# Three ScalarE instructions and eight matmuls at other steps of a hand-written step table (layer 2 of a four-layer image kernel)

## Chip, cores, metric

The kernel runs on one core of one Trainium2 chip. The metric is the device time of one execution in microseconds (us). The kernel before takes 7983.3 us (median of three runs, 7979.73 to 7997.88).

## What is computed

An image of 2 x 64 x 96 x 96 numbers (fp32) goes through four layers. Layer 0 is a non-local attention block over the 9216 positions, layer 3 a filter whose taps depend on the image's mean. Between them stand five selective state-space scans ("Mamba" blocks): one in layer 1, over each image as one sequence, and four in layer 2. Layer 2 has two halves; each runs a forward and a backward block over the image's rows or columns as short sequences of 96:

```python
def _block(u, p):
    return _mamba(_rmsnorm(u, p['norm_w']), p) + u
def _bimamba(u, pf, pb):
    yf = _block(u, pf)
    yb = jnp.flip(_block(jnp.flip(u, 1), pb), 1)
    return jnp.concatenate([yf, yb], axis=-1)
...
# in _mamba: x = silu(conv(in_proj(u))); dt, B, C from x; then over time, per channel d and state s:
h = dA * h + dt_t[:, :, None] * B_t[:, None, :] * x_t[:, :, None]   # dA = exp(dt * A)
y = einsum('nds,ns->nd', h, C_t)
```

The norm of layer 2 is x times the inverse root of the mean of its squares over 64 channels. The forward and the backward block of a pair read the same normalized image.

## The kernel before

**Units and steps.** Layers 1 and 2 are cut into 120 units of 768 positions: 24 units of layer 1, then 96 of layer 2, which come in 48 pairs, a forward and a backward unit of the same eight sequences. The first 24 pairs are layer 2's first half, the others its second. A unit's states, 128 channels by 16 states, take 16 steps; a step handles 128 rows in two turns of 384 positions. The first eight steps are the unit's first 384 positions, the other eight its second, so a unit has two "halves" of B.

**One step** (`run`, from L955). SyncE issues two transfers of 384 KB that spread rows of dt and of dt times x over the partitions (`read`, L846), five steps ahead. ScalarE makes the decay, two exponentials of 128x384 (`decay`, L853), three steps ahead. VectorE multiplies the spread rows by B into PSUM (`inputs`, L863; two steps' worth at every even step) and runs the scan (`scan`, L878). GpSimd multiplies the states by C (L879). TensorE sums the states into y (`gather`, L888), two steps behind or more. Below, "placement s" is L863 of step s, "product s" is L879 of step s.

**B.** One PSUM bank holds B for one half (`shared`, L857). The matmul of the second half is recorded in step 6, behind placements 6 and 7, which are the last to read the first half's B; that of the next unit's first half in step 14, behind placements 14 and 15.

**The step table.** Everything else of a unit is a list of pieces, `PIECES` (L930): (offset in steps from the unit's start, method). The pieces of later units run between the steps of the one being scanned. In every step, `run` records first the reads, the decay, the placement and scan, `shared` and the gathers, then the pieces that are in `reads` (L961), then the others, each group in the table's order. What is recorded is the order of each engine's queue: the whole runs under a manual schedule. Buffers come from pools; a piece that needs a new buffer waits until the old one's last reader is done. One two-bank PSUM buffer (`m`) serves all pieces of TensorE in turn.

**The pieces around the change**, with the step at which each falls and the unit that is then being scanned:

| piece | line | engine, work | step |
|---|---|---|---|
| `norm_square`, layer 2 | L714, L715 | ScalarE: two copies of the image (64x768 each, to both halves of the partitions), one square of 128x768 | 15 of a forward unit, for the pair after next; in `reads` |
| `norm_mean`, `norm_root` | L693, L723 | TensorE mean, ScalarE log and exp | 1 and 3 of a backward unit |
| `norm_scale` | L737 | GpSimd | 10 of a backward unit |
| `conv` | L755, L761 | TensorE: four taps by two halves, 16 records | 5, every unit, for the unit after next |
| `conv_read` | L766 | ScalarE | 7 |
| `gate_mm`, `gate_read` | L693, L772 | TensorE, ScalarE | 7, 9 |
| `y_half` | L892 | ScalarE: copy of the first half of y | 10 |
| `silu` | L775, L776 | ScalarE: table load, silu, table load | 10 |
| `tail_0`, `tail_1`, `tail_read` | L671, L924 | TensorE: the previous pair's output, ScalarE copies it to the image | 9, 10, 11 of a forward unit |
| `step_mm`, `step_read`, `step_exp` | L671, L792 to L799 | TensorE, ScalarE: towards dt of the next unit | 11, 13, 14 |
| `step_kept`, `step_sum`, `step_dt`, `step_u` | L806 to L816 | GpSimd: dt and dt times x | 15, 1, 5, 7 |
| `step_write` | L825 | SyncE: two transfers of 768 KB, the rows of the next unit | 8 |

SyncE's queue holds `step_write` between the reads of step 13 and those of step 14: `read` runs five steps ahead, and `step_write` is recorded in step 8 after that step's reads. Layer 1 has its own form of the norm (`u.carry`), one per unit.

Of the kernel before, what the change touches and what calls it, by code (L numbers as in the profile page):

```python
# [20 lines left out]
AF = mybir.ActivationFunctionType  # L21
# [10 lines left out]
D_STATE, DT_RANK, D_CONV = 16, 4, 4  # L32
HALF = 4 * W
CH = 2 * HALF
# [33 lines left out]
def rows_of(b):  # L68
    return slice(b * C, (b + 1) * C)
# [551 lines left out]
class Mamba:  # L621
# [79 lines left out]
            u.p = self.mm([(self.t.centre[rows_of(u.b)], self.halves(u.image))])  # L701

    def norm_square(self, u):
        if u.norm.unit is not u:
            return
        u.norm.x = self.work("xn", D_CONV - 1 + CH)
        u.sq = self.work("sq", bufs=1)
        x = u.norm.x[:, D_CONV - 1 :]
        if u.carry:
            self.nc.scalar.activation(u.sq, u.p, AF.Square)  # L710
            self.nc.scalar.copy(x, u.p)
        else:
            for j in range(2):
                self.nc.scalar.copy(x[rows_of(j)].rearrange("p (n t) -> p n t", n=u.image.shape[1]), u.image)  # L714
            self.nc.scalar.activation(u.sq, x, AF.Square)  # L715

    def norm_mean(self, u):
        if u.norm.unit is u:
# [197 lines left out]
    def tail_read(self, u):  # L916
# [10 lines left out]


    PIECES = (
        (-51, "norm_centre"),  # L930
        (-49, "norm_square"),
        (-47, "norm_mean"),
        (-45, "norm_root"),
        (-38, "norm_scale"),
        (-36, "norm_affine"),
        (-27, "conv"),
        (-25, "conv_read"),
        (-25, "gate_mm"),
        (-23, "gate_read"),
        (-22, "silu"),  # L940
        (-21, "step_mm"),
# [25 lines left out]
    def run(self, units, first, n_first, other):  # L967
# [8 lines left out]
        table = [[] for _ in range(self.STEPS)]  # L976
        for offset, name in self.PIECES:
            table[offset % self.STEPS].append((name not in reads, offset, name))
        begin, end = self.PIECES[0][0], self.PIECES[-1][0]


        self.nc.scalar.preload_act_table_set("natural_log_exp_and_others")
        first(0)
        for offset, name in self.PIECES:
            if offset < 0:
# [326 lines left out]
```

## Time and profile before

| | busy us | share of 7974.9 us |
|---|---|---|
| TensorE | 7063.0 | 89% |
| VectorE | 6749.1 | 85% |
| ScalarE | 5214.3 | 65% |
| GpSimd | 4724.4 | 59% |

These shares mix stages. Layer 0 takes about the first 2700 us; layer 1's units are scanned from 2732 to 3821 us, layer 2's from 3821 to 7890 us, layer 3 is the rest. From 5882 to 7890 us VectorE is busy 1934.15 of 2008 us, GpSimd 1825.96, TensorE 1697.87, ScalarE 1511.72, and the 16 DMA engines have a mean share of 0.90. So in layer 2 VectorE sets the pace, and what it waits for is what can be gained. The unit of account in the text below is the pair: two units, some 84 us, 48 times.

A row of the timeline is: start, duration, engine, line, operation, tiles written and read, form, count; then the engine's idle time before it, and who ended it.

### The profile page before, as it was taken

The page shows a single profiled execution, that of the slowest core. Times are in us where ns is not written, and L with a number is a line of the kernel's source. Part 1 is how long each engine was busy: PE and PEld are TensorE (multiplying, and loading weights), DVE is VectorE, ACT ScalarE, POOL GpSimd, SP SyncE. Part 2 cuts the span into 40 slices and gives each one's busy share as a digit, 9 for nine tenths or more (in the row PEclk, how much of TensorE's full clock was granted, in tenths as well). Part 3 has the DMA queues.
Part 4 walks back from the last instruction along what each step waited for, and adds up shares of the span by engine and source line. Part 5 has one row for each costly group of instructions (what it writes and reads, how often), then busy time and mean ns, then how long its engine had stood idle before and what let it go on. Part 6 is the DMA issues. An engine that isn't in the chain of part 4 may idle for free.

```text
span 7974.9 us, 82275 instructions
## 1 busy us (share of the span) xinstructions
PE 7063.0 (89%) x24578; PEld 3122.4 (39%) x24578; DVE 6749.1 (85%) x5524; ACT 5214.3 (65%) x6953; POOL 4724.4 (59%) x3146
## 2 busy tenths in 40 slices
PE   9999999999999788888888888888888888888887
PEld 3333333333333344444444444444444444444443
DVE  6666666666666599999999999999999999999999
ACT  4444444444444577777777777777777777777773
POOL 0000000000000399999888889989889999999985
PEclk9999999999999899999999999999999999999999
DMA  1000000000000388888888888988998899898985
GB/s 43 1 1 1 1 1 1 3 5 5 5 5 3 144 303 317 312 304 325 312 332 325 328 329 329 342 334 328 334 337 334 340 341 347 336 336 335 343 335 205
DMA packets 593806, 1726.06 MB, mean 216 GB/s; under 512 B 65988, under 2 KB 67140, under 8 KB 592840
## 3 DMA queue, kind: packets, MB, share of 16 engines
q1 hardware_dynamic: 591904, 1717.68, 57.9%
q8 instruction: 196, 3.21, 0.2%
q10 hardware_dynamic: 1448, 3.05, 0.1%
q14 instruction: 258, 2.11, 0.1%
HBM read 1522.68 MB, written 197.79 MB: 216 GB/s over the span
## 4 chain that ended last, share of the span: by engine, by line
PE 11%; DMA 10%; ACT 9%; issue 8%; POOL 8%; DVE 4%; SPq 1%; DVEq 0%; ACTq 0%; POOLq 0%
DMA spread<-rows 7%; PE y L888 6%; POOL h L879 6%; ACT h L853 3%; DMA rows<-dtu 3%; PE mm L671 2%; DVE place L863 2%; DVE h L878 1%; PE conv L761 1%; POOL dtu L812 1%; POOL dtu L816 1%; PE y L885 1%; DVE xa L1211 1%; ACT xn L714 1%; PE mm L693 1%
## 5 line engine op out<-in xcount | busy, mean ns | idle before, releaser
L879 POOL TENSOR_TENSOR h<-h,C 128x768 f32<-128x768 f32 x1920 | 3452.4, 1817 | 347.4 <-DVE h L878 310.3
L888 PE MATMUL y<-h,pair 128*128 128x384 f32 x7680 | 2809.6, 510 | 103.4 <-POOL h L879 102.7
L878 DVE TENSOR_TENSOR_SCAN h<-h,place 128x768 f32<-128x768 f32 x1536 | 2606.3, 1737 | 13.6 <-ACT h L853 13.0
L888 PEld LDWEIGHTS y<-h,pair 128*128 128x128 f32 x7680 | 1513.6, 200 | 1306.8 <-POOL h L879 239.6
L311 ACT ACTIVATE e<-f_exp 128x1536 f32<-128x1536 f32 x864 | 1206.4, 1448 | 1224.4 <-PE f_exp L301 1224.4
L853 ACT ACTIVATE h<-spread,xa 128x384 f32<-128x384 f32 x3072 | 1734.3, 608 | 367.0 <-DMA spread<-rows 343.6
L367 DVE TENSOR_TENSOR acc_e<-acc_e,e 128x1536 f32<-128x1536 f32 x792 | 1389.9, 1755 | 683.7 <-ACT e L311 644.8
L863 DVE TENSOR_TENSOR place<-spread,B 128x768 f32<-128x768 f32 x1920 | 1735.0, 948 | 261.9 <-PE B L857 250.8
L340 POOL TENSOR_TENSOR xa<-xa,t_att 64x512 f32<-64x512 f32 x36 | 45.3, 1259 | 2612.3 <-ACT t_att L338 2612.3
L318 PE MATMUL y_att<-e,xb 128*64 128x512 f32 x5184 | 1243.7, 601 | 0.0
L301 PE MATMUL f_exp<-theta,phi 64*128 64x512 f32 x5184 | 1234.6, 607 | 1.0 <-DVE xb L284 0.5
L301 PEld LDWEIGHTS f_exp<-theta,phi 64*128 64x128 f32 x5184 | 466.4, 186 | 754.5 <-issue 460.6
L874 DVE TENSOR_TENSOR_SCAN h<-h,state,place 128x384 f32<-128x384 f32 x768 | 714.0, 990 | 0.0
L318 PEld LDWEIGHTS y_att<-e,xb 128*64 128x64 f32 x5184 | 341.6, 136 | 830.5 <-issue 829.2
L853 ACT ACTIVATE h<-spread,rates 128x384 f32<-128x384 f32 x768 | 433.0, 608 | 150.3 <-DMA spread<-rows 137.5
L885 PE MATMUL y<-raw,xa 128*128 128x384 f32 x384 | 220.4, 663 | 210.5 <-ACT yg L895 182.8
L671 PE MATMUL mm<-raw,xa 128*128 128x384 f32 x768 | 301.2, 517 | 99.2 <-ACT xb L924 91.5
L766 ACT ACTIVATE raw<-conv,cols 128x768 f32<-128x768 f32 x120 | 108.2, 902 | 305.2 <-PE conv L761 240.9
L806 POOL TENSOR_TENSOR kept<-dtu,kept 128x768 f32<-128x768 f32 x120 | 218.3, 1819 | 118.4 <-ACT kept L799 117.9
L761 PE MATMUL conv<-xn,xa 64*128 64x384 f32 (+3 forms) x1536 | 273.1, 494 | 11.7 <-DVE xa L1093 4.0
L892 ACT COPY yg<-y 128x384 f32<-128x384 f32 x120 | 57.4, 478 | 289.7 <-PE mm L671 205.1
L857 PE MATMUL B<-raw,xa 128*128 128x384 f32 x384 | 170.7, 526 | 83.8 <-DVE place L863 83.7
(206 smaller groups left out, 5434.3 us busy)
## 6 DMA issues: line engine op xcount, KB each, us to landing
spread<-rows SPq DMA_DIRECT2D x3840, 384.0 KB, 6.4
rows<-dtu SPq DMA_DIRECT2D x240, 768.0 KB, 5.9
image<-pre SPq DMA_DIRECT2D x11, 384.0 KB, 2.3
xb<-image SPq DMA_DIRECT2D x11, 384.0 KB, 5.8
xa<-in_x SPq DMA_DIRECT2D x1, 2304.0 KB, 23.1
out<-xa ACTq DMA_DIRECT2D x7, 240.0 KB, 2.0
out<-xa SPq DMA_DIRECT2D x1, 1200.0 KB
xa<-in_x SPq DMA_DIRECT2D x3, 384.0 KB, 11.6
```

The source lines that it names most:

```text
L301: nc.tensor.matmul(fs[j // 3][:, bass.ts(j % 3, NB)], lhsT=phi[at, bass.ts(m // 2, P)], rhs=theta[at, bass.ts(i, NB)], start=True, stop=True,)
L311: nc.scalar.activation(e, f, AF.Exp)
L318: nc.tensor.matmul(y[rows_of(m % 2)], lhsT=g[:, m, :], rhs=es[j // 3][:, bass.ts(j % 3, NB)], start=m < 2, stop=m >= KEYS - 2,)
L367: nc.vector.tensor_add(acc, acc, e)
L671: self.nc.tensor.matmul(o, lhsT=lhsT, rhs=x, start=n == 0, stop=n == len(terms) - 1)
L761: self.nc.tensor.matmul(p3[:, :, o], lhsT=lhsT, rhs=x3[:, :, i], **flags)
L853: self.nc.scalar.activation(h[:, bass.ts(q, HALF)], dt, AF.Exp, scale=u.w.rates[:, n : n + 1])
L863: self.nc.vector.tensor_mul(bx, x, self.B.unsqueeze(1).to_broadcast([P, 2, HALF]))
L874: nc.vector.tensor_tensor_scan(h[:, at], h[:, at], bx[:, at], state[:, q : q + 1], ALU.mult, ALU.add)
L878: nc.vector.tensor_tensor_scan(h[:, way], h[:, way], bx[:, way], 0.0, ALU.mult, ALU.add)
L879: nc.gpsimd.tensor_mul(h2, h2, u.C[:, bass.ts(half, HALF)].unsqueeze(1).to_broadcast([P, 2, HALF]))
L888: self.nc.tensor.matmul(self.y, lhsT=self.t.gather[n], rhs=rhs, start=False, stop=stop)
```

## The change

```diff
     def norm_square(self, u):
-        if u.norm.unit is not u:
-            return
-        u.norm.x = self.work("xn", D_CONV - 1 + CH)
-        u.sq = self.work("sq", bufs=1)
-        x = u.norm.x[:, D_CONV - 1 :]
         if u.carry:
+            u.norm.x = self.work("xn", D_CONV - 1 + CH)
+            u.sq = self.work("sq", bufs=1)
             self.nc.scalar.activation(u.sq, u.p, AF.Square)
-            self.nc.scalar.copy(x, u.p)
-        else:
-            for j in range(2):
-                self.nc.scalar.copy(x[rows_of(j)].rearrange("p (n t) -> p n t", n=u.image.shape[1]), u.image)
-            self.nc.scalar.activation(u.sq, x, AF.Square)
+            self.nc.scalar.copy(u.norm.x[:, D_CONV - 1 :], u.p)
+
+    def image_copy(self, u, j):
+        if u.norm.unit is u and not u.carry:
+            x = u.norm.x[rows_of(j), D_CONV - 1 :].rearrange("p (n t) -> p n t", n=u.image.shape[1])
+            self.nc.scalar.copy(x, u.image)
+    def image_0(self, u):
+        if u.norm.unit is u and not u.carry:
+            u.norm.x = self.work("xn", D_CONV - 1 + CH)
+        self.image_copy(u, 0)
+    def image_1(self, u):
+        self.image_copy(u, 1)
+    def image_square(self, u):
+        if u.norm.unit is u and not u.carry:
+            u.sq = self.work("sq", bufs=1)
+            self.nc.scalar.activation(u.sq, u.norm.x[:, D_CONV - 1 :], AF.Square)
...
     PIECES = (
+        (-56, "image_0"),
+        (-52, "image_1"),
+        (-52, "image_square"),
         (-51, "norm_centre"),
...
-        (-27, "conv"),
-        (-25, "conv_read"),
-        (-25, "gate_mm"),
+        (-26, "conv"),
+        (-24, "conv_read"),
+        (-24, "gate_mm"),
         (-23, "gate_read"),
```

For layer 2, the first image copy goes from step 15 of a forward unit to step 8 of the same unit, the second copy and the square to step 12; all three now stand behind that step's `reads` pieces. For every unit, the convolution goes from step 5 to step 6, where `shared` is recorded before it; its read and the gate's matmul go from step 7 to step 8. `gate_read` stays in step 9. No instruction is added or taken away. On TensorE's queue the order "gather 3, convolution, B, gather 4" becomes "gather 3, B, gather 4, convolution"; on ScalarE's the copy and the square of step 12 stand between the decay of step 12 and that of step 13, ahead of `step_read` and `step_exp`. The first copy of the first layer-2 pair takes a buffer whose last reader is `norm_scale` of the last layer-1 unit, which GpSimd does in step 10, two steps after the copy's own.

## The prediction

> **What bounds the kernel now.** I first looked at the busy time by stretch: in layer 2 VectorE is busy 96% of the time, so I read who ends its waits there (waits of VectorE, 3821 to 7890 us: who, for whom, total us, times, longest):
>
> ```profile
> DVE place L863 <- PE B L857: 137.1, 84, 3.2
> DVE h L878 <- ACT h L853: 13.0, 17, 1.7
> DVE place L863 <- DMA spread<-rows: 9.6, 16, 1.1
> ```
>
> Nearly all is placement waiting for B. Sorted by step over VectorE's timeline, 57.7 us stand before placement 0 of backward units, 73.4 us before placement 8 of backward units, 6.0 us before placement 8 of forward ones. Two waits per pair, then, with different causes. I follow the pair that starts at 5288.96; A is its forward unit, B its backward unit, scanned from 5331.50. VectorE:
>
> ```profile
> 5331.50 1.82 DVE L863 TENSOR_TENSOR place<-spread,B 128x768 f32<-128x768 f32 x2 [2.32 <-PE B L857]
> ...
> 5353.98 1.83 DVE L863 TENSOR_TENSOR place<-spread,B 128x768 f32<-128x768 f32 x2 [2.31 <-PE B L857]
> ```
>
> Without a wait two steps take 5.02 us (from one placement pair to the next), a unit 40.2. TensorE in the same pair:
>
> ```profile
> 5303.25 2.82 PE L761 MATMUL conv<-xn,xa 64*128 64x384 f32 x16
> 5305.99 0.91 PE L857 MATMUL B<-raw,xa 128*128 128x384 f32 x2
> ...
> 5324.98 2.35 PE L671 MATMUL mm<-raw,xa 128*128 128x384 f32 x4 [1.92 <-ACT xb L924]
> 5327.12 3.69 PE L888 MATMUL y<-h,pair 128*128 128x384 f32 x8
> 5330.65 0.81 PE L857 MATMUL B<-raw,xa 128*128 128x384 f32 x2
> ...
> 5350.29 2.81 PE L761 MATMUL conv<-xn,xa 64*128 64x384 f32 x16
> 5353.03 0.91 PE L857 MATMUL B<-raw,xa 128*128 128x384 f32 x2
> ```
>
> The wait at placement 8 (5353.98) is the convolution in front of B: it is worth 2.74 us (start of `conv` to start of `B`). The wait at placement 0 (5331.50) has another cause: `step_mm` waits for `tail_read`, and the gathers and B stand behind it. In A the convolution costs nothing: it fills the time until placement 7, which B must wait for, ends at 5305.81. ScalarE and GpSimd:
>
> ```profile
> 5317.63 0.48 ACT L892 COPY yg<-y 128x384 f32<-128x384 f32 x1 [5.04 <-PE mm L671]
> 5323.36 1.57 ACT L924 ACTIVATE xb<-mm,cols 64x768 f32<-64x768 f32 x1
> 5328.22 0.89 ACT L793 ACTIVATE dtu<-mm,cols 128x768 f32<-128x768 f32 x1
> 5331.75 0.94 ACT L799 ACTIVATE kept<-kept,minus 128x768 f32<-128x768 f32 x1
> 5333.73 3.11 ACT L714 COPY xn<-xb 64x768 f32<-64x768 f32 x2
> 5367.48 0.61 ACT L853 ACTIVATE h<-spread,xa 128x384 f32<-128x384 f32 x1 [0.78 <-DMA spread<-rows]
> ```
>
> ```profile
> 5332.77 1.82 POOL L806 TENSOR_TENSOR kept<-dtu,kept 128x768 f32<-128x768 f32 x1 [1.57 <-ACT kept L799]
> 5335.12 3.60 POOL L879 TENSOR_TENSOR h<-h,C 128x768 f32<-128x768 f32 x2 [0.54 <-DVE h L878]
> 5356.53 0.11 POOL L820 MEMSET dtu<- 128x8 f32 x1
> ```
>
> `y_half` stood idle 5.04 us for TensorE's tail, so everything of ScalarE behind it in A (silu, `tail_read`, `step_read`, `step_exp`) hangs on when TensorE reaches the tail. GpSimd's `kept` waits for the end of `step_exp`, and from its first product in B to the end of `step_u` it does not pause. Only then does SyncE issue the rows (5356.67), and behind them the reads of steps 14 and 15; the last of these lands 10.8 us later, when ScalarE's row of 5367.48 starts. Placement 15 needs that transfer; here it starts at 5369.92 and does not wait, because the wait at placement 8 has pushed it back by 2.31 us.
>
> [...] `kept` idles 1.57 us at the head of GpSimd's queue with products behind it. [...] behind 1.92 us of waiting, 12 matmuls from 5324.98 take 5.67 us (start to start of B), against 0.32 us each in steady gathers.
>
> **The change, part by part** (durations from the pair above; the sum is made against the profiled span of 7974.9 us, 8.4 below the median of the three runs).
>
> 1. *B ahead of the convolution, in B units.* B no longer waits for 2.74 us of convolution. The 73.4 us go, and the 6.0 us of forward units.
>
> 2. *The same in A units.* TensorE gets there at 5303.25, that is A+14.29, but B must wait for placement 7 until A+16.92. The convolution that filled this time now comes after it. From `conv` to `y_half` TensorE's packed work is 13.53 us in this half of layer 2 where no wait falls in it (14.38 in this pair, two waits for GpSimd within), 12.91 in the second half; its contents do not change. So `y_half` comes at A+16.92+13.53 = 30.45, against 28.67: 1.8 later. Over all pairs `y_half` is now at A+28.9 (first half) and A+29.2 (second, where the earliest possible becomes 29.8): on average 1.5 and 0.7 later, a little more where TensorE comes later than 16.92.
>
> 3. *First copy at step 8 of A.* 1.45 us in the first half, 0.83 in the second, on ScalarE between `conv_read` and the decay. It is hidden in the 5.04 us before `y_half`. `gate_read`, now one step behind its matmul, falls into the same idle time. In B units and in layer 1 `y_half` may come 0.5 to 1.5 us later; there ScalarE then waits for transfers (2 to 3 us before the decay of step 14 in layer 1), which hides it: nothing.
>
> 4. *Second copy and square at step 12 of A.* 1.56+0.84+0.03 = 2.43 us (first half), 1.74 (second), ahead of `step_read` and `step_exp`, less 0.3 to 0.7 of ScalarE's waits for transfers that they fill. Behind them on the queue: the decays of steps 0 and 1 (slack of some steps), `step_read`, `step_exp`; who waits for these: GpSimd's `kept`, and all its products behind it.
>
> 5. *What they leave at step 15:* ScalarE no longer has 3.95 us of copies between the decays of steps 2 and 3 of B. The 13.0 us of waits for the decay go. `y_read` and `norm_mean` stay about where they are, since the same work now stands earlier.
>
> **The sum.** End of `step_read` in A: 30.45 + 5.73 (to `tail_read`, as now) + 1.59 + 1.1 (decay) + 2.43 + 1.1 + 1.68 = 44.08, against 40.15. The end of `step_exp` follows 3.58 later as now: 47.66, against 43.73. GpSimd: 23.4 from there to the rows' issue (seen in every backward unit where `kept` is late): 71.1, against 67.7. Last transfer of step 15: 10.2 to 10.8 later, 81.3 to 81.9; then 0.12, and 4.18 from placement 15 to the next pair: 85.6 to 86.2. The pair takes 85.0 on average now (pairs 11 to 24, from the start of one to that of the next), so 0.6 to 1.2 more. The wait at placement 8 is thus replaced by two: a longer one at placement 0 of B, and a new one at placement 15 of B for the rows. Second half, with its terms: 29.83 + 5.77 + 0.97 + 1.1 + 1.74 + 1.1 + 1.68 + 3.58 + 23.4 + 10.2 to 10.8 + 4.3 = 83.7 to 84.3 where TensorE is in time at A+16.92, against 83.74 on average; as it often isn't (the convolution starts at A+16.07 on average, and up to 18.4), I add 0.3. I take 0.9 for 14 pairs, 0.7 for 24, and 0.5 for the first ten, where VectorE's own weight preparation (2.7 us a pair) hides some: 12.6 + 16.8 + 5 = 34 us.
>
> Once, at the border of the layers, the first copy waits for GpSimd's `norm_scale` two steps on: ScalarE stands still for up to 10 us in layer 1's chain. Bounds: 0, if its later waits for transfers (3 us a unit) and slack take it up, and 12; a gain is excluded, since nothing gets earlier. I take 8. Sum 42 us: 7983.3 + 42 = 8025.
>
> The unknown: whether the pause of TensorE before B in A (0 to 2.6 us, new) drops its clock. Between nothing[...] and 1.9 us (six matmuls at 0.64) in half the forward units, 48/2 x 1.9 = 46 us. I take nothing; the upper end goes into the range.
>
> **Rivals.** *The rows have slack* (ends faster): if `step_exp` ends by B+2.0, the rows land before placement 15 would come, and the 79.4 + 13.0 us of waits are simply gone, less what placement 0 gains: 7983 - 92 = 7891, or 7930 if the 1 us at placement 0 stays on (48 x 0.8). For it: in some pairs now (B units with no wait at 8) the rows are in time. Against: there `step_exp` ends at B+1.0, and the change puts it some 3.9 us later (43.73 to 47.66), of which a later start of B takes back about 1. The point from which it decides is B+2.0. Chance 0.15. *It cancels*: the pair stays at its length within 0.3 us, 7983 +- 16. For it: the least values of the sum above (85.5 and 83.5) give 14 x 0.5 - 24 x 0.2, nearly nothing. Chance 0.17. *Clock*: the pause drops TensorE's clock, 8025 + 46 = 8071. Chance 0.13. My forecast, the rows' chain: 0.55.
>
> **The numbers.** 8025 us is the likeliest case, alone 7999 to 8060. A measurement of this kernel can tell 0.2% (16 us) from no change. Faster 0.15, same 0.17, slower 0.55 + 0.13 = 0.68. The range leaves out most of the faster case and the far end of the clock's: 7955 to 8080.
>
> **What would show it.** Right: no wait for B at placement 8; waits for B at placement 0 of backward units of 2 to 3 us on average; a new wait of 1 to 2.5 us for `spread` at placement 15 of backward units; `kept` ending 1 to 2 us later in B; layer 1 as before. Wrong: the rows issued before B+25.7, no wait at placement 15, and `y_half` of A before 29.8.

## The result and the profile after

The changed kernel takes **8027.6 us** (median of four runs, 8027.27 to 8042.47), the kernel before 7981.5 on the same chip: a ratio of 1.0058, 95% interval 1.0040 to 1.0075. It is 46 us slower. The profiled executions have spans of 7974.9 and 8026.0 us, 51 us apart; the sums by stage and by step below are of these two. Below, A+18.2 is a time 18.2 us after the start of the forward unit A of a pair.

First the waits of all engines in layer 2 (engine, line, who ended the wait: us, times, longest), cut to the rows that answer to those of before. The lines of the changed kernel lie 14 further down: placement is L877, the decay L867, B L871.

```profile
ACT h L867 <- DMA spread<-rows: 415.3, 885, 3.6
...
DVE place L877 <- DMA spread<-rows: 133.2, 134, 3.6
...
DVE place L877 <- PE B L871: 70.8, 43, 3.4
...
DVE h L892 <- ACT h L867: 7.9, 9, 2.1
```

VectorE's waits for B fell from 137.1 to 70.8 us, and its waits for transfers rose from 9.6 to 133.2. ScalarE's decays waited 343.3 us for transfers before and 415.3 now. Sorted by step over VectorE's timeline: the 79.4 us at placement 8 are gone, as are the 13.0 us at scan 3; 69.6 us of waits for B stand before placement 0 of backward units (57.7 before); and of the waits for transfers 77.9 us fall in backward units (74.3 of them at placements 14 and 15) and 55.3 in forward ones, against 0.8 and 8.9. With the scan's waits for the decay, VectorE waits 212 us for these three, against 160: the 52 us more are about what layer 2 grew by (54 us to the start of its last unit).

VectorE in one pair (A starts at 5481.02, B at 5525.03; same columns as in the prediction):

```profile
5518.19 0.96 DVE L877 TENSOR_TENSOR place<-spread,B 128x768 f32<-128x768 f32 x1 [1.04 <-DMA spread<-rows]
5521.39 1.75 DVE L892 TENSOR_TENSOR_SCAN h<-h,place 128x768 f32<-128x768 f32 x1 [0.59 <-ACT h L867]
5525.03 1.83 DVE L877 TENSOR_TENSOR place<-spread,B 128x768 f32<-128x768 f32 x2 [1.89 <-PE B L871]
5561.81 0.96 DVE L877 TENSOR_TENSOR place<-spread,B 128x768 f32<-128x768 f32 x1 [1.50 <-DMA spread<-rows]
5564.12 0.96 DVE L877 TENSOR_TENSOR place<-spread,B 128x768 f32<-128x768 f32 x1 [1.35 <-DMA spread<-rows]
```

No wait is left at placement 8. The wait at placement 0 is there as before, and the transfers are late in both units, not in B alone. TensorE in the same pair:

```profile
5490.42 1.65 PE L899 MATMUL y<-raw,xa 128*128 128x384 f32 x2 [5.20 <-ACT yg L909]
...
5499.25 0.81 PE L871 MATMUL B<-raw,xa 128*128 128x384 f32 x2
5501.28 2.82 PE L775 MATMUL conv<-xn,xa 64*128 64x384 f32 x16
...
5520.21 1.56 PE L671 MATMUL mm<-raw,xa 128*128 128x384 f32 x4 [1.90 <-ACT xb L938]
5524.18 0.81 PE L871 MATMUL B<-raw,xa 128*128 128x384 f32 x2
```

B now precedes the convolution. It comes at A+18.2 and not at A+16.9: TensorE has waited 5.20 us for `y_read` (L909) before it (265.6 us of such waits in layer 2, 182.8 before). ScalarE and GpSimd, through the pair:

```profile
5512.87 0.48 ACT L906 COPY yg<-y 128x384 f32<-128x384 f32 x1 [3.29 <-PE mm L671]
...
5518.60 1.55 ACT L938 ACTIVATE xb<-mm,cols 64x768 f32<-64x768 f32 x1
5520.18 1.12 ACT L867 ACTIVATE h<-spread,xa 128x384 f32<-128x384 f32 x2
5521.32 1.56 ACT L716 COPY xn<-xb 64x768 f32<-64x768 f32 x1
5522.92 0.84 ACT L729 ACTIVATE sq<-xn 128x768 f32<-128x768 f32 x1
5523.67 1.10 ACT L867 ACTIVATE h<-spread,xa 128x384 f32<-128x384 f32 x2
5524.80 0.90 ACT L806 ACTIVATE dtu<-mm,cols 128x768 f32<-128x768 f32 x1
...
5529.13 0.94 ACT L813 ACTIVATE kept<-kept,minus 128x768 f32<-128x768 f32 x1
...
5560.81 0.61 ACT L867 ACTIVATE h<-spread,xa 128x384 f32<-128x384 f32 x1 [1.71 <-DMA spread<-rows]
5561.71 0.61 ACT L867 ACTIVATE h<-spread,xa 128x384 f32<-128x384 f32 x1 [0.29 <-DMA spread<-rows]
5563.02 0.61 ACT L867 ACTIVATE h<-spread,xa 128x384 f32<-128x384 f32 x1 [0.70 <-DMA spread<-rows]
...
5565.98 0.62 ACT L867 ACTIVATE h<-spread,xa 128x384 f32<-128x384 f32 x1 [0.30 <-DMA spread<-rows]
5566.50 0.88 ACT L806 ACTIVATE dtu<-mm,cols 128x768 f32<-128x768 f32 x1
...
5570.82 0.94 ACT L813 ACTIVATE kept<-kept,minus 128x768 f32<-128x768 f32 x1
```

```profile
5530.15 1.82 POOL L820 TENSOR_TENSOR kept<-dtu,kept 128x768 f32<-128x768 f32 x1 [5.11 <-DVE h L892]
5531.92 3.59 POOL L893 TENSOR_TENSOR h<-h,C 128x768 f32<-128x768 f32 x2
...
5551.41 1.83 POOL L830 TENSOR_TENSOR dtu<-dtu,raw 128x768 f32<-128x768 f32 x1
5553.31 0.11 POOL L834 MEMSET dtu<- 128x8 f32 x1
```

Read these two fences as one **closed loop**. In A, the tail's copy (5518.60), the second image copy and the square stand one behind the other ahead of `step_read` (5524.80). `step_exp` ends at 5530.07, B+5.04. GpSimd's `kept` follows at once (5530.15; its row names a scan, which ended at the same moment, but in all 47 pairs measured `kept` starts 0.08 us behind the end of `step_exp`), and GpSimd is done with the rows at 5553.42. SyncE issues them at 5553.44. The rows need two transfers of 3.03 us each (the median from the landing of one transfer to that of the next), and every read behind them 0.98 us. That is why ScalarE's six decays of 5560.81 to 5566.6 wait for one transfer after the other: steps 14 and 15 of B, and step 0 of the next unit. `step_read` of the next A stands behind them (5566.50). So `step_exp` ends at 5571.76, which is 3.46 us into the next A. It ended near A+0.9 in this half of layer 2 before. From there the late `step_exp` delays A's own rows, and also the copy of y (`y_read`, A+8.9 against A+6.4), and with that TensorE's next gathers (the 5.20 us above), its convolution and its tail. Then the turn begins again. From the end of `step_exp` that falls in A (5484.53) to the one that falls in B it takes 45.54 us, and from there to the one in the next A 41.69: together 87.2, about the length of this pair. The sum alone proves no loop, since whatever comes once a pair recurs after a pair's length. That the links have no slack, and so set this length, is for the experiments to show.

### The profile page after: what moved, and what is told of

Its sections match the earlier page's. It is cut to its first block, busy times and chain, and to the rows that moved or that the text cites. A ratio compares the mean times of both kernels' runs of the same rounds, so it can differ in the third digit from the quotient of the medians.

```text
span 8026.0 us, 82232 instructions
## 1 busy us (share of the span) xinstructions
PE 7085.6 (88%) x24578; PEld 3112.3 (39%) x24578; DVE 6759.4 (84%) x5524; ACT 5218.9 (65%) x6953; POOL 4718.9 (59%) x3146
## 4 chain that ended last, share of the span: by engine, by line
PE 15%; DMA 13%; POOL 12%; ACT 10%; issue 8%; DVE 4%; SPq 1%; DVEq 0%; ACTq 0%; POOLq 0%
DMA spread<-rows 9%; POOL h L893 9%; PE y L902 8%; ACT h L867 4%; DMA rows<-dtu 3%; PE mm L671 3%; PE conv L775 2%; DVE place L877 1%; POOL dtu L830 1%; PE B L871 1%; POOL dtu L826 1%; DVE xa L1228 1%; DVE h L892 1%; POOL yg L912 1%; PE y L899 1%
## 5 line engine op out<-in xcount | busy, mean ns | idle before, releaser
L902 PE MATMUL y<-h,pair 128*128 128x384 f32 x7680 | 2858.6, 514 | 71.6 <-POOL h L893 69.9
L867 ACT ACTIVATE h<-spread,xa 128x384 f32<-128x384 f32 x3072 | 1748.5, 608 | 450.7 <-DMA spread<-rows 416.0
L877 DVE TENSOR_TENSOR place<-spread,B 128x768 f32<-128x768 f32 x1920 | 1742.2, 949 | 309.3 <-PE B L871 174.4
L867 ACT ACTIVATE h<-spread,rates 128x384 f32<-128x384 f32 x768 | 433.0, 608 | 91.9 <-DMA spread<-rows 79.2
L899 PE MATMUL y<-raw,xa 128*128 128x384 f32 x384 | 223.6, 672 | 304.2 <-ACT yg L909 265.6
L871 PE MATMUL B<-raw,xa 128*128 128x384 f32 x384 | 169.1, 523 | 114.0 <-DVE place L877 113.8
L899 PEld LDWEIGHTS y<-raw,xa 128*128 128x128 f32 x384 | 69.6, 227 | 439.4 <-ACT yg L909 327.7
```

What stands on the lines that cost most here:

```text
L867: self.nc.scalar.activation(h[:, bass.ts(q, HALF)], dt, AF.Exp, scale=u.w.rates[:, n : n + 1])
L877: self.nc.vector.tensor_mul(bx, x, self.B.unsqueeze(1).to_broadcast([P, 2, HALF]))
L902: self.nc.tensor.matmul(self.y, lhsT=self.t.gather[n], rhs=rhs, start=False, stop=stop)
```

## Experiments

Each experiment changes only offsets in the step table, unless its diff says otherwise. The kernel before ran beside each group: medians 7981.4, 7979.3, 7979.2 and 7979.2.

**1. The convolution alone** (the kernel before, with the convolution's three pieces moved):

```diff
-        (-27, "conv"),
-        (-25, "conv_read"),
-        (-25, "gate_mm"),
+        (-26, "conv"),
+        (-24, "conv_read"),
+        (-24, "gate_mm"),
```

> Only the convolution's three pieces move (steps 6, 8, 8); the three ScalarE instructions stay at step 15 of A. Rows' chain: step_exp of A loses the 2.43/1.74 us of copy and square in front of it, so in B it ends near B+2.3 instead of B+4.6 to 5.0 (first half) and 4.05 (second); the rows then land just about when placement 15 of B is due. The 78 us of DMA waits of B units shrink to some 15, the 55 us of A units stay, the 13 us at scan 3 come back, the 79 us at placement 8 are gone: 8027 - 63 + 13 + 8 less at the border's end = 7965 to 7990, about as before. Rival (TensorE reaches the tail later, and that alone is the cost): taking the images back changes nothing there, 8020 to 8040.

Measured: 7962.8 us, ratio 0.9976 (0.9969 to 0.9984). Moving the convolution alone is no loss but a small gain, and in the profiled executions, 14 us apart, all of it lies in layer 1: its first 20 units take 898.4 us against 912.0. In layer 2 the pair keeps its length (84.88 and 83.74 us in the rest of the first half and in the second, against 85.03 and 83.74). The waits at placement 8 fall from 79.4 to 1.3 us, and 61.7 us of waits for rows and 17 more at placement 0 stand in their place.

**2. The images alone** (the changed kernel, with the three lines above taken back):

> Only the images and the square move (steps 8, 12, 12 of A); the convolution stays in step 5. Rows' chain: step_exp ends at about B+3.4 and B+2.7 instead of B+1.0, the rows land near B+37.5, and placement 15 of B comes at B+38.4 because the wait at placement 8 is still there: hidden. The 13 us at scan 3 go, 8 us at the border of the layers come: 7970 to 7990. Rival (2.43/1.74 us ahead of step_exp are paid in every pair, whatever the convolution does): 48 x about 1 us, 8020 to 8040.

Measured: 8022.7 us, ratio 1.0055 (1.0042 to 1.0069). My expectation was wrong, and the rival's number is right: the images alone cost nearly all that the whole change costs. The timelines of VectorE and, behind the second half of B, of ScalarE in this kernel (B starts at 5527.58) show why the slack at placement 15 didn't help:

```profile
5527.58 1.83 DVE L877 TENSOR_TENSOR place<-spread,B 128x768 f32<-128x768 f32 x2 [1.68 <-PE B L871]
5549.90 1.83 DVE L877 TENSOR_TENSOR place<-spread,B 128x768 f32<-128x768 f32 x2 [2.15 <-PE B L871]
5566.38 0.96 DVE L877 TENSOR_TENSOR place<-spread,B 128x768 f32<-128x768 f32 x1 [0.45 <-DMA spread<-rows]
```

```profile
5559.40 1.28 ACT L790 ACT_TABLE_LOAD   x1
5563.39 0.62 ACT L867 ACTIVATE h<-spread,xa 128x384 f32<-128x384 f32 x1 [2.70 <-DMA spread<-rows]
...
5568.62 0.62 ACT L867 ACTIVATE h<-spread,xa 128x384 f32<-128x384 f32 x1 [0.71 <-DMA spread<-rows]
5569.15 0.88 ACT L806 ACTIVATE dtu<-mm,cols 128x768 f32<-128x768 f32 x1
```

In this pair VectorE hardly waits for the rows (0.45 us), and its wait at placement 8 is still there. But ScalarE waits 2.70 us for them before a decay, and `step_read` stands behind the decays. The rows were late for ScalarE, which needs each step three steps before VectorE does. Over layer 2 the cost does show in VectorE's waits, for rows and for B (9.6 and 137.1 us before):

```profile
DVE place L877 <- PE B L871: 151.2, 118, 3.5
...
DVE place L877 <- DMA spread<-rows: 47.9, 67, 2.1
```

**3. The rows behind the reads** (the changed kernel with `step_write` at step 10):

```diff
-        (-8, "step_write"),
+        (-6, "step_write"),
```

> The changed kernel, with step_write at step 10 instead of step 8, so that on SyncE's queue the reads of steps 13, 14 and 15 stand ahead of the rows and don't wait for GpSimd. Rows' chain: the 133 us of DMA waits at placements 14 and 15 go almost wholly; some 20 to 60 us come back before placement 0, where the next unit's rows or B are then due earlier. 7900 to 7970. Rival (TensorE and ScalarE set the pair's length, and the waits at 15 only stand where placement 0 would wait else): the waits move to placement 0, 8015 to 8035.

Measured: 7891.9 us, ratio 0.9888 (0.9873 to 0.9903), that is 136 us less than the changed kernel; 21 us of it lie in layer 1 (1084.0 to 1062.9), the rest in layer 2. The rival falls. VectorE's waits in layer 2, and ScalarE where the six decays stood (B starts at 5459.98):

```profile
DVE place L877 <- PE B L871: 80.1, 43, 3.6
DVE h L892 <- ACT h L867: 23.1, 32, 2.5
DVE place L877 <- DMA spread<-rows: 7.7, 4, 2.1
```

```profile
5494.00 2.64 ACT L867 ACTIVATE h<-spread,xa 128x384 f32<-128x384 f32 x5
5497.74 0.61 ACT L867 ACTIVATE h<-spread,xa 128x384 f32<-128x384 f32 x1 [1.10 <-DMA spread<-rows]
5498.27 0.88 ACT L806 ACTIVATE dtu<-mm,cols 128x768 f32<-128x768 f32 x1
```

Of 133.2 us of waits for rows 7.7 are left, five of the six decays run without a wait, and `step_read` starts at B+38.3, not B+41.5.

**4. The second copy and the square one step behind the first copy** (the changed kernel):

```diff
-        (-52, "image_1"),
-        (-52, "image_square"),
+        (-55, "image_1"),
+        (-55, "image_square"),
```

> The changed kernel, with the second copy and the square at step 9 instead of 12, so all three stand ahead of y_half, where ScalarE is idle for TensorE's tail (some 5 us; they take 3.9 and 2.6). Rows' chain: step_exp of A ends 2.4/1.7 us earlier, B+2.3; the 78 us of DMA waits of B units go down to some 15 to 25, those of A units stay: 7960 to 7985. Rival (copies cost wherever they stand, or TensorE alone is the cause): 8015 to 8040.

Measured: 7961.0 us, ratio 0.9974 (0.9964 to 0.9985). That is what the convolution alone takes (7962.8): the same work on the same engine, put ahead of `y_half` where ScalarE is idle for TensorE's tail, costs nothing against its old place. It is the place between `tail_read` and `step_read` that costs 67 us, not the copies.

**5. The rows behind the reads, in the kernel before** (the diff of 3):

> The kernel before, with step_write at step 10 instead of 8. Closed loop (step_exp, rows, late reads of steps 13 to 15, ScalarE's decays of these steps, step_read of the next unit behind them): before is not on it, its waits are at placements 0 and 8, and only 10 us of VectorE's waits are for rows. Some 10 us there and up to 17 us in layer 1: 7945 to 7975. Rival (the place of step_write is worth 135 us in any kernel, whatever the images do): 7835 to 7860.

Measured: 7909.8 us, ratio 0.9914 (0.9901 to 0.9928). This lies between both expectations. Of the 81 us by which its profiled execution is shorter, layer 1 gives 49 (1088.6 to 1039.4 us), layer 2's second half 32 (a pair from 83.74 to 82.33), the first half nothing to speak of (85.03 to 85.29 in pairs 11 to 24). (This execution is the fastest of the five: 7895.7 us.) So the rows already held back the kernel before in those two stretches, though VectorE waited only some 10 us for them. In layer 1 ScalarE's waits for rows fell from 137.8 to 84.2 us; in the second half they stayed (184.3 and 182.9 us), so a sum of waits alone doesn't tell what a bound is worth. VectorE's waits for B in layer 1, 45 us without the one at its start, are gone. TensorE's granted clock in layer 1 also rose, from 0.95 to 0.98; whether that followed from the shorter waits or brought a part of the gain itself was not tried.

**6 and 7. The rows behind the reads**, with the images of 4, and with the convolution alone of 1:

> The changed kernel with both: second copy and square at step 9, step_write at step 10. Closed loop: the 82 us of waits for rows that are left with the images at 8 and 9 go, and with them some 10 us of layer 1: 7961 - 82 x 0.9 - 10 = 7865 to 7890. Rival (with step_write at step 10 the loop is cut, so the place of the images no longer matters): 7884 to 7900, as with step_write alone.

> The kernel before with the convolution at step 6 and step_write at step 10; the images stay at step 15. Closed loop: of the convolution alone, 62 us of waits for rows go, and some 15 us of layer 1: 7963 - 55 - 15 = 7880 to 7905. Rival (VectorE's waits go from placement 15 to placement 0, since TensorE is what is late): 7945 to 7965.

Measured: 7891.1 us, ratio 0.9890 (0.9875 to 0.9905), and 7902.6, ratio 0.9907 (0.9892 to 0.9922). In 6 the rival is right: with the convolution at step 6 and the rows out of the way, the place of the second copy is worth nothing (7891.1 against 7891.9), where it is worth 67 us with the rows at step 8. In 7, 60 us go with the rows, as expected.

**8. The square twice** (the changed kernel; the result is the same):

```diff
             self.nc.scalar.activation(u.sq, u.norm.x[:, D_CONV - 1 :], AF.Square)
+            self.nc.scalar.activation(u.sq, u.norm.x[:, D_CONV - 1 :], AF.Square)
```

> The changed kernel with the square of step 12 done twice (the same result), 0.85 us more on ScalarE ahead of step_read, once per pair. Closed loop: the copies lie on it at full price, the pair grows by 0.85: 48 x 0.85 = 41 us, 8055 to 8075. Rival (slack in front of step_read takes it up, the loss has another cause): 8020 to 8035.

Measured: 8066.6 us, ratio 1.0109 (1.0093 to 1.0124). These 39 us are 48 times 0.81, for a square of 0.84: what stands there is paid at nearly full price on average. By stretch it is not even: in the profiled executions a pair grows by 1.23 us in the first ten, 0.84 in pairs 11 to 24 and 0.61 in the second half.

**9. The images alone, with the rows behind the reads** (2 and 3 together):

> The convolution at step 5 as before, the images and the square at steps 8, 12, 12 of A, step_write at step 10. Loop through the rows: the 41 us that the images alone cost are paid only by way of the late rows, so they vanish; what is left is the kernel before with step_write at step 10 (7910) and up to 9 us at the border of the layers, less 11 us at scan 3: 7900 to 7925. Rival (the copies delay step_exp, y_read and so TensorE's convolution and tail of A, with no rows needed for it): the 41 us stay, 7940 to 7960.

Measured: 7850.4 us, ratio 0.9836 (0.9822 to 0.9849). The 41 us that the images alone cost with the rows at step 8 have turned into a gain of 59 (against 7909.8). The rival falls, and my expectation was too careful. With the copies no longer at step 15, `y_read` of B comes at B+9.2 instead of B+11.6, the convolution of B at 16.4 instead of 19.7 (medians of pairs 11 to 24), and the waits at placement 8 go from 74.8 to 36.2 us although the convolution still stands in front of B. VectorE in layer 2 of this kernel:

```profile
DVE place L877 <- PE B L871: 84.2, 66, 2.8
```

**10. The rows between the reads of steps 14 and 15** (the changed kernel with `step_write` at step 9):

> The changed kernel with step_write at step 9: the reads of step 14 stand ahead of the rows, those of step 15 behind them. After the rows' issue the transfers run one behind the other, two of 3.1 us for the rows and 0.97 us for each read, so step 15 lands 1.95 us earlier than in the changed kernel, W+8.3 instead of W+10.2. Loop through the rows: twice 1.95 a pair is more than the 2.6 that the changed kernel's pair lies above that with step_write at step 10, so most of the 135 us comes: 7895 to 7920. Rival (the price is paid in proportion to the bytes behind the rows, half of it stays): 7945 to 7970.

Measured: 7915.5 us, ratio 0.9916 (0.9903 to 0.9930): five sixths of what step 10 gives, as was expected of the loop.

**11 and 12. A version that beats both**: images at 8, 9 and 9, convolution at step 5, rows at step 10; and the same with the first pair of layer 2 left at step 15 (in its table pieces a flag of this pair skips the copies, and `norm_square` makes them):

```diff
-            if u.norm.unit is u and not u.carry:
+            if u.norm.unit is u and not u.carry and not u.norm.old:
...
+        elif u.norm.unit is u and u.norm.old:
+            u.norm.old = False
+            self.image_0(u)
+            self.image_1(u)
+            self.image_square(u)
```

> The convolution back at step 5, the second copy and the square at step 9, step_write at step 10. If copy and square at step 12 still delay y_read of B (it is at B+9.0 there) and through it the convolution and placement 8, moving them ahead of y_half takes away most of the 36 us of waits at placement 8: 7815 to 7840. Rival (with the rows out of the way the place of the second copy is worth nothing, as with the convolution at step 6): 7842 to 7860.

> The same, but the first pair of layer 2 keeps its copies and square at step 15, so that ScalarE doesn't stand for the norm_scale of the last unit of layer 1. If the border of the layers (units 20 to 24) is lengthened by that wait, 8 to 11 us less than the run before it. Rival (that wait is taken up by slack, and the border's length comes from something else): the same within 3 us.

Measured: 7815.5 us, ratio 0.9786 (0.9773 to 0.9800), and **7803.8 us, ratio 0.9782 (0.9769 to 0.9796)**. In 11 the rival falls: with the convolution at step 5 the place of the second copy and the square is worth 35 us (against 7850.4), where with the convolution at step 6 it was worth nothing. Between 11 and 12 the two intervals overlap; the stage tells them apart: units 20 to 24 take 181.7 us in 11 and 172.2 in 12. In all nine profiles with the first pair's copies moved these units take 181.7 to 187.8 us, in the five without 172.2 to 177.5.

All places of the convolution and the images against the two places of the rows (medians, us; the place with a dash was not run):

| | rows at step 8 | rows at step 10 |
|---|---|---|
| as before | 7981.5 | 7909.8 |
| convolution at step 6 | 7962.8 | 7902.6 |
| images at 8, 12, 12 | 8022.7 | 7850.4 |
| both: the changed kernel | 8027.6 | 7891.9 |
| images at 8, 9, 9, convolution at 6 | 7961.0 | 7891.1 |
| images at 8, 9, 9, convolution at 5 | - | 7815.5 |

The change is a loss of 46 us in the left column and a gain of 18 in the right one.

The loop can be measured in each trace: from the end of `step_exp` that falls in A to the one that falls in B ("A part", which holds TensorE's tail and the copies), and from there to the one in the next A ("B part", which holds the rows). Means of pairs 11 to 24, us:

| | A part | B part | sum |
|---|---|---|---|
| before | 42.87 | 42.21 | 85.08 |
| convolution alone | 42.75 | 42.23 | 84.99 |
| images alone | 44.53 | 41.78 | 86.31 |
| the changed kernel | 44.77 | 41.69 | 86.46 |
| with the square twice | 45.60 | 41.70 | 87.30 |
| with images at 8, 9, 9 | 42.78 | 41.83 | 84.61 |
| with rows at step 9 | 44.96 | 39.56 | 84.51 |
| with rows at step 10 | 45.14 | 38.63 | 83.77 |

With the rows at step 8 the B part never falls below 41.7: 23.4 from `step_exp` to the rows' issue, 13.0 from there to `step_read`, 5.3 to the end of `step_exp` (in the changed kernel). That floor gives way only where the rows move. The A part takes up the copies (1.7 to 2.0 of their 2.4 us) and the doubled square (0.83 of 0.85), and is hardly touched by the convolution. Neither part has slack: the pair follows where the B part alone is shortened (rows at step 9 or 10) and where the A part alone is changed (images at 8, 9, 9, or the square twice).

## Why the prediction was right, and where not

Sign, size and chain were right: 42 us slower was forecast and 46 measured, by way of copies ahead of `step_exp`, GpSimd, the rows and the transfers of step 15. Its parts did not all hold, and the size is in part luck.

*Step 1* (placement 8 falls free) came as written: no wait of the 79.4 us is left.

*Step 2* (B ahead of the convolution puts `y_half` of A 1.8 later, and the pair pays for it together with the copies) is **the step that failed**. `y_half` does come at A+31.1 (30.45 was forecast). But the wait before placement 0 of B, where this was to show, is 1.5 us on average (1.2 before), and not 2 to 3. The convolution alone leaves the A part and the pair as they were, and with the images alone, the convolution still at step 5, `y_half` comes at A+30.9 as well, because `y_read` is late. I had counted from placement 7 of A, as if every pair started afresh. The pair's length is a turn of the loop, and there only work between `tail_read` and `step_exp`, or in the B part, counts. The 1.8 becomes visible once the rows and the copies are both out of the way: with the images at 8, 9 and 9 and the rows at step 10, the convolution in step 6 costs 76 us (7815.5 to 7891.1); in pairs 11 to 24 `y_half` of A goes from A+28.7 to 30.6 and the pair from 81.94 to 84.06. With the images at 8, 12 and 12 it costs 42 us (7850.4 to 7891.9), and the waits for B at placement 0 of B go from 48.1 to 80.1 us; but a third of this lies in layer 1, and in pairs 11 to 24 the pair grows by 0.2 only, though `y_half` of A goes from A+28.8 to 31.3. With the images at step 15 it costs nothing (7909.8 to 7902.6). Why it is hidden there was not tried.

*Step 3* (first copy hidden ahead of `y_half`) held; experiment 4 hid even all three there.

*Step 4* (2.43 us on the chain) was the cause, at 1.7 to 2.0 of it. It doesn't need the lost wait at placement 8, as the prediction had it: the images alone cost 41 us with that wait still in place.

*Step 5*: the scan's waits at step 3 went as forecast, and `y_read` in B stayed about where it was (B+10.7 to B+10.2). In A, which the step does not speak of, it went from A+6.4 to A+8.9.

*The sum* came near for all that: in pairs 11 to 24 `step_exp` ends at A+48.1 (47.66 forecast), and the rows are issued at A+71.5 (71.1). The late `y_read` brought the lateness of `y_half` that the convolution was to bring.

*The pairs*: 1.39, 0.98 and 1.2 us longer (pairs 11 to 24, the second half, the first ten) where 0.9, 0.7 and 0.5 were put: 55 us, not 34. The missing term is A's own late rows, 55.3 us of waits in A (all but 0.2 at placements 14 and 15), which the prediction did not have. *The border* cost 9.3 (units 20 to 24: 176.6 to 185.9 us; 8 was put). ScalarE stands there for 5.81 us in layer 1, idle before the first image copy until GpSimd's `norm_scale` is done.

*Layer 1* was put at nothing and gained 13.9 us in its first 20 units, as with the convolution alone (13.6). ScalarE's waits for rows in that layer fell from 137.8 to 79.9 us. With the rows at step 10 the convolution's place gains nothing there (867.0 to 877.7 us), so the gain hangs on the rows; by which link was not tried. Other runs repeat both: with the rows at step 8 these units take 910.4 and 912.0 us with the convolution at step 5, and 895.2 to 898.4 in the four with it at step 6; with the rows at step 10 it is 867.0 to 877.9 and 877.7 to 881.1. The two misses, 21 too little in the pairs and 14 too much in layer 1, cancelled for the most part: without that luck the forecast would have been too low.

*The rivals.* "The rows have slack" asked for `step_exp` before B+2.0; it ends at B+4.8 (median of pairs 11 to 24). The clock case did not come: in the 47 forward units the convolution's 16 records took no longer behind B than before (2.35 us from first to last start, both), and the pause that the case needs stood before B (over 0.1 us) in only 6 of them. Nor does the granted clock go with the loss: in the first and the second half of layer 2 it was 0.95 and 0.95 before, 0.94 and 0.95 with the change, 0.93 and 0.94 with the convolution alone, where the pair kept its length, and 0.95 and 0.94 with the images alone, where it grew. "It cancels" is what the convolution alone does in layer 2.

*The order on GpSimd's queue.* Step 4 has all of GpSimd's products wait behind `kept`. The 1.57 us that `kept` stood idle in the pair of the prediction don't show it, because the product behind `kept` wasn't ready either: it waited 0.54 us more for its own scan. The changed kernel shows it: the scan of step 0 of B had ended at 5528.51, but GpSimd stood idle until `kept` began at 5530.15, and the product came only behind it, at 5531.92. On ScalarE the square done twice shows the like: with 0.85 us more ahead of it, `step_exp` closes the A part 0.83 us later (45.60 against 44.77).

## What to carry to other kernels

Look for waits on every queue that a late transfer passes, not only on the busiest engine: with the images alone VectorE waited 0.45 us for the rows in the pair shown where ScalarE waited 2.70, and what stood behind ScalarE's decays closed a loop in which late work made the next work late. When a queue of transfers holds a store that waits for an engine, first put the loads that don't need it ahead: one number in the table turned a loss of 46 us into a gain of 89 over the kernel before. The price of moving a piece holds only for the bound of that moment: the same images cost 41 us or gained 59, by where the rows stood, and the same convolution gained 19 with rows and images at their old places or cost 42 with both moved.

## What was not expected of the hardware

The rows' store of 768 KB takes 3.03 us from landing to landing, a read of 384 KB 0.98 us: 259 against 402 GB/s, worked out from 786,432 and 393,216 bytes. So two stores hold up the queue about as long as six reads do, 6.06 against 5.88 us. No run here shows why a store moves fewer bytes in a microsecond than a read does.

The wait of TensorE for `tail_read` (a median of 1.92 us before, 1.86 after) is followed by a slow stretch in 21 of 47 pairs before and in 11 of 46 after: the four matmuls of `step_mm` and the eight gathers behind them take 5.67 us instead of 3.97 (medians), and TensorE's granted clock falls to 0.50 within each of these stretches, where it stays at 1.00 in all the others. In the pair that the prediction shows, five of the twelve lie 0.64 us apart, and the last ones 0.32; from 5326.30 to 5328.90 the granted clock is 0.50. No wait under 1.85 us was followed by it (0 of 16 before, 0 of 23 after; in all fourteen profiles 0 of 322); of the waits from 1.85 us on, 21 of 31 and 11 of 23 were (146 of 328). So behind a wait of about 1.9 us the clock is sometimes halved for a while and sometimes not, and no run here shows why. Short and long waits also come in different pairs of the layer, so whether the length itself decides was not tried.
